# Keeping an order for PE and DVE in the first two attention blocks, products of ones in PE's first waits, and gathered blocks late in the banks of the scores

## The chip, the cores and the metric

The kernel runs on one core of one Trainium2 chip. The time is the device time of one execution in microseconds. Before the change the median of three runs is 336.43 us (335.42 to 338.63). A profile is one more execution, recorded by the hardware.

The engines are named as in the profile: PE multiplies matrices, PEld is its load of the stationary operand, DVE works on vectors and reduces, ACT evaluates functions and copies, POOL does element-wise work and issues indirect DMAs, SP issues most other DMAs. SPq, ACTq, POOLq and PEq are their queues of instructions.

## The reference

A tensor x of shape (2, 1024, 256) passes through four residual steps, in float32. The context has 77 rows of 192 numbers for each of the two batches.

```python
x = x + L0_xattn(layernorm(x), ctx)   # 16 heads of 16, softmax over 77 keys
x = x + L0_ffn(layernorm(x))          # 256 -> 1024 -> 256, relu; then a layernorm
x = x + L1_xattn(layernorm(x), ctx)   # one head of 256
x = x + L1_ffn(layernorm(x))          # one of 8 matrices 256x256 for each position
```

In the first ffn only expert 0 counts, since its router weights are set to one for expert 0 and to zero for the others. In the last step the matrix of a position is the argmax of a product of its position code with the signs of `tile_sigs`: it depends on the position and the inputs, not on x.

## The kernel before

The 2048 rows of x are cut into eight chunks of 256 rows (`c` = 0 to 7), and each chunk into two blocks of 128 rows for the first attention (`b` = 0 to 15). The first four chunks are batch 0, the others batch 1. A chunk goes through four generators:

- `attention0` takes moments of x (`st_a`, `mv_a`, the root on POOL as `rs_a`, `sh_a`), normalizes on ACT (`n_a`), transposes on PE (`ps_xT_a`, copied by ACT to `xT_a`), forms `qT` by `ps_q`, and begins two blocks. `attention0_block` forms scores of all 16 heads in `sc`, a tile of four PSUM banks from the pool `ps2`, which has one buffer. DVE takes the maximum (`mx`) and subtracts it (`pr`) for each half of the heads, ACT takes the exponential, DVE sums (`sm`), takes reciprocals, and ACT spreads them (`sme`). PE transposes `pr` and `sme` in three banks of four (`ps_pT`), ACT copies them (`pT`), PE multiplies by the values (`ps_o<-pT,vbd`), DVE scales (`oT`), PE projects (`ps_y<-wo,oT`), and DVE adds to x.
- `ffn0` normalizes again (`n_f`), transposes, forms four pairs of hidden tiles (`ps_h`, `hT`), and sums them for the two blocks (`ps_eo`), and does the layernorm (`st_g`, `tb`).
- `attention1` is the second attention (`n_b`, `xT_b`, `ps_s`, `ps_pT1`, `ps_y` by `vo`).
- `to_slots` normalizes (`mv_h`, `rs_h`) and scatters the rows to `slots`, a buffer in HBM for each batch that is sorted by matrix, so that a block of 128 slots needs one matrix. The last chunk doesn't go there: `by_every_tile` multiplies it by all eight matrices (`ps_z`) and keeps the right one.

`block(e, j, place)` handles block j of 128 slots of batch e; there are 15 for batch 0 and 13 for batch 1. SP loads its matrix (`wt`, four buffers; for batch 1 ahead of time into the places of `vbd`, `w1`, `w2`) and its rows (`blk`, six buffers). PE transposes the rows (`ps_yT`), ACT copies (`yT`), PE multiplies (`ps_t`), DVE adds the bias (`res`), and POOL scatters to the output (`out<-res,blk`). Both PSUM tiles come from the pool `ps1`, which has four banks and serves all other products.

The order is set in two layers. Each generator yields places, numbers on a common scale of chunks, and `run` takes the generators from a heap by place. Within `run`, the instructions of the engines that are named in `ordered` keep the order in which they are issued; those of other engines, and all of them in a later `run` without names, are placed by the planner of the programming layer. It also adds every semaphore, and gives each engine one fixed order of instructions. Before the change DVE alone keeps its order, for places below 0.

Other generators in the first stage are `first_context` (keys: `ps_cxT`, `ps_k`, `kbd`), `values` (`ps_v`, the masked values `vbd`), `row_of_biases` (`bvb`, `ps_bv`, into `rows`), and `choices` (the matrix of each position; it needs `sigT` and `peT`). DMAs in `loads` that are issued late wait for the first transposes of chunk 0, done["a0"].

## Time and profile before

| | |
|---|---|
| median of three runs | 336.43 us |
| the profiled execution, its own time | 340.51 us |
| its span, first to last instruction | 338.4 us |
| PE busy | 301.8 us, 89%, 2144 instructions |
| DVE busy | 211.0 us, 62% |
| ACT busy | 141.4 us, 42% |
| POOL busy | 130.6 us, 39% |
| mean granted clock of PE | 0.967 |
| chain that ended last: PE, DVE, issue, DMA | 63%, 18%, 7%, 4% |
| moved by DMA | 39.69 MB, mean 117 GB/s |

The page shows the span in 40 slices of 8.46 us; a digit is the busy share of an engine in tenths, and PEclk the granted clock in tenths of full speed. A line of the timeline reads: start, busy time, engine, line of the kernel, operation, what it writes and reads, shapes, how often, and in brackets the idle time of the engine before it with what released it. Each float32 matmul that is not a transpose appears as two instructions. Matmuls are pipelined and their ends are modelled.

### The profile page before, as it was taken

The numbers are of one execution on the slowest core, as the hardware profiler recorded it, in microseconds if no ns is written. First come the engines' busy times: TensorE is split into PE (matmuls) and PEld (weight loads), VectorE is DVE, ScalarE is ACT, GpSimd is POOL, SyncE is SP. The second block draws the span as 40 slices with busy tenths as digits, with TensorE's granted clock in tenths as the row PEclk, the third lists the DMA queues.
The fourth block names the chain that finished last, engine by engine and source line by source line (L and its number), as shares of the span: only waits on it lengthen the run. The fifth ranks groups of instructions, "written<-read, shape, count | busy, mean of one in ns | idle before, by whom it ended". The sixth has DMA issues, their size and how long they took to land.

```text
span 338.4 us, 6080 instructions
## 1 busy us (share of the span) xinstructions
PE 301.8 (89%) x2144; PEld 247.6 (73%) x2144; DVE 211.0 (62%) x624; ACT 141.4 (42%) x309; POOL 130.6 (39%) x183
## 2 busy tenths in 40 slices
PE   2979789999799899999999999999799996578995
PEld 2656568888488678877887888888688885455884
DVE  2278884695459657929757784894346659326343
ACT  2246566535234457365464744645324421212110
POOL 3104560424003458346435512432652716415422
PEclk9999999999899999999999999999999999559999
DMA  7597299999401302701000100250845687164510
GB/s 198 197 334 184 104 241 139 213 158 76 39 0 44 115 13 93 255 32 45 20 2 0 64 0 2 69 182 1 252 133 183 204 253 254 64 186 128 167 34 16
DMA packets 23209, 39.69 MB, mean 117 GB/s; under 512 B 2669, under 2 KB 9354, under 8 KB 23180
## 3 DMA queue, kind: packets, MB, share of 16 engines
q1 hardware_dynamic: 19788, 32.22, 38.3%
q0 software_dynamic: 2848, 6.57, 5.9%
q10 hardware_dynamic: 544, 0.52, 0.5%
q8 instruction: 17, 0.28, 0.4%
q14 instruction: 12, 0.10, 0.1%
HBM read 25.52 MB, written 15.62 MB: 122 GB/s over the span
## 4 chain that ended last, share of the span: by engine, by line
PE 63%; DVE 18%; issue 7%; DMA 4%; POOL 3%; ACT 2%; SPq 1%; POOLq 0%; ACTq 0%
PE ps_eo L688 15%; PE ps_h L676 11%; PE ps_t L809 5%; PE ps_pT L634 4%; PE ps_z L834 4%; PE ps_y L656 4%; DVE mx L608 3%; PE ps_q L580 3%; DVE pr L610 3%; PE ps_o L643 2%; PE ps_s L721 2%; PE sc L599 2%; PE ps_y L746 2%; DMA wt<-in_wrow 2%; DMA wk<-in_wk 2%
## 5 line engine op out<-in xcount | busy, mean ns | idle before, releaser
L676 PE MATMUL ps_h<-xT_f,w 128*128 128x256 f32 x256 | 63.3, 390 | 3.0 <-issue 2.1
L688 PE MATMUL ps_eo<-w,hT 128*128 128x256 f32 x256 | 58.4, 381 | 1.9 <-ACT hT L681 1.9
L676 PEld LDWEIGHTS ps_h<-xT_f,w 128*128 128x128 f32 x256 | 47.0, 192 | 11.6 <-issue 4.5
L688 PEld LDWEIGHTS ps_eo<-w,hT 128*128 128x128 f32 x256 | 47.5, 190 | 8.3 <-ACT hT L681 2.3
L173 POOL DMA_INDIRECT out<-res,blk x28 | 27.4, 980 | 38.1 <-DVE res L814 14.5
L681 ACT ACTIVATE hT<-ps_h,cols 128x256 f32<-128x256 f32 x64 | 27.1, 466 | 30.7 <-PE ps_h L676 30.6
L614 ACT ACTIVATE pr<-pr 128x616 f32<-128x616 f32 x32 | 22.9, 717 | 37.5 <-DVE pr L610 37.5
L608 DVE TENSOR_REDUCE mx<-sc 128x8 f32<-128x616 f32 x32 | 25.2, 788 | 5.3 <-PE sc L599 5.3
L635 ACT COPY pT<-ps_pT 128x512 f32<-128x512 f32 x48 | 25.4, 595 | 6.2 <-PE ps_pT L634 6.2
L750 DVE SCALAR_TENSOR_TENSOR x<-ps_y,sm,x 128x256 f32<-128x256 f32 x16 | 7.1, 479 | 29.7 <-PE ps_y L746 29.7
L617 DVE TENSOR_REDUCE sm<-pr 128x8 f32<-128x616 f32 x32 | 24.6, 781 | 1.4 <-ACT pr L614 1.0
L610 DVE TENSOR_TENSOR pr<-sc,mx 128x616 f32<-128x616 f32 x32 | 25.2, 787 | 0.2
L805 ACT COPY yT<-ps_yT 128x256 f32<-128x256 f32 x28 | 10.4, 371 | 35.2 <-PE ps_yT L803 35.2
L634 PE MATMUL ps_pT<-ident,pr 128*128 128x128 f32 x160 | 21.0, 274 | 3.7 <-ACT pr L614 2.0
L566 POOL TENSOR_TENSOR x<-x,rows 128x512 f32<-128x512 f32 x16 | 21.0, 1321 | 8.3 <-ACT n_a L227 5.4
L634 PEld LDWEIGHTS ps_pT<-ident,pr 128*128 128x128 f32 x160 | 18.1, 141 | 5.9 <-ACT pr L614 2.5
L656 PE MATMUL ps_y<-wo,oT 128*128 128x256 f32 x64 | 17.4, 394 | 4.5 <-DVE oT L650 4.5
L765 POOL TENSOR_TENSOR both<-x,bias 128x256 f32<-128x256 f32 x14 | 9.9, 725 | 24.6 <-DVE x L750 24.5
L643 PE MATMUL ps_o<-pT,vbd 128*32 128x128 f32 x512 | 19.0, 283 | 0.1
L643 PEld LDWEIGHTS ps_o<-pT,vbd 128*32 128x32 f32 x512 | 14.4, 112 | 5.7 <-issue 4.5
L809 PE MATMUL ps_t<-wt,yT 128*128 128x256 f32 x60 | 16.9, 403 | 1.8 <-ACT yT L805 1.3
L173 POOL DMA_INDIRECT slots<-both,to x14 | 14.3, 1019 | 9.2 <-DVE both L232 2.7
(196 smaller groups left out, 545.8 us busy)
## 6 DMA issues: line engine op xcount, KB each, us to landing
blk<-slots SPq DMA_DIRECT2D x28, 256.5 KB
slots<-zero SPq DMA_DIRECT2D x1, 3847.5 KB
wt<-in_wrow SPq DMA_DIRECT2D x15, 256.0 KB
slots<-zero SPq DMA_DIRECT2D x1, 3334.5 KB
w<-in_w SPq DMA_DIRECT2D x2, 1024.0 KB
every<-in_wrow SPq DMA_DIRECT2D x1, 2048.0 KB
wt_w<-in_wrow SPq DMA_DIRECT2D x8, 256.0 KB
x<-in_x SPq DMA_DIRECT2D x7, 256.0 KB
```

The lines of the kernel that those rows point to most:

```text
L173: i = nc.gpsimd.indirect_dma_start(out=to, out_offset=bass.IndirectOffsetOnAxis(ap=index, axis=0), in_=rows_in, in_offset=None, bounds_che ...
L608: nc.vector.tensor_reduce(mx, scv, AX.X, ALU.max)
L610: nc.vector.tensor_tensor(p8.rearrange("p (j h l) -> p j h l", j=4, l=L), scv, mx.unsqueeze(3).to_broadcast([P, 4, 2, L]), ALU.subtract,)
L617: nc.vector.tensor_reduce(sm[:, g * 8 : g * 8 + 8], pr[:, g, :G8].rearrange("p (h l) -> p h l", l=L), AX.X, ALU.add,)
L634: nc.tensor.transpose(ps[:, j * P : (j + 1) * P], srcs[4 * n + j], ident)
L635: nc.scalar.copy(pT[:, n].rearrange("p j t -> p (j t)"), ps)
L643: nc.tensor.matmul(ps[32 * m : 32 * m + 32, g * P : (g + 1) * P], vbd[:, e, n, g, 32 * m : 32 * m + 32], pTs[:, g * NK + n, :], start=n == ...
L656: nc.tensor.matmul(ps[:, :D], oT[:, g, :], wo[:, g, :], start=g == 0, stop=g == KC - 1)
L676: nc.tensor.matmul(ps[:, j, :], w1[:, k, (f + j) * P : (f + j + 1) * P], tT[:, k, :], start=k == 0, stop=k == KC - 1,)
L681: nc.scalar.activation(hT[-1][:, j, :], ps[:, j, :], AF.Relu, bias=col(C_B1 + f + j))
L688: nc.tensor.matmul(ps[:, :D], hT[f // 2][:, f % 2, i * P : (i + 1) * P], w2[:, f, :], start=f == 0, stop=f == F // P - 1,)
L809: nc.tensor.matmul(ps[:, :D], yT[:, k * P : (k + 1) * P], w[:, k * D : (k + 1) * D], start=k == 0, stop=k == KC - 1,)
```

## The change

It moves and adds work and removes none of the results.

- PE and DVE both keep the order of issue, for all places below 1 instead of DVE for places below 0. Places of the first two chunks' generators are set by hand: `attention0(1)`, blocks 0 and 1 (`FIRST`), `values`, `row_of_biases`; `ffn0(0)` is placed 1.2 earlier.
- `warm` multiplies `ones` by itself 7, 5 and 2 times at three early places.
- In each block of the first attention the transposes of `pr` (banks 0 and 1) are placed ahead of the sums, and bank 2, with `sme`, after them.
- The load of `sigT` goes from SP's queue to ACT's.
- A block of slots no longer takes two banks from `ps1`. All 28 blocks use one tile `spare`, the four banks of the scores after their last use: block after block takes the next bank, transposes into its first half and multiplies into its second. Blocks of batch 0 are placed from 19.9 on, in steps of 0.1, instead of 16.0 in steps of 0.32. For batch 1 the place of the transposes is unchanged.

```diff
+    sigT = load("sigT", [NP, NT], a["sigT"], nc.scalar)
...
-    sigT = load("sigT", [NP, NT], a["sigT"])
...
+    def warm(n):
+        ps = bank(f"warm_{next(number)}")
+        for _ in range(n):
+            nc.tensor.matmul(ps[:, :P], ones, ones, start=True, stop=True)
...
     def attention0(c, x):
-        yield 2 * c - 1.8
+        at = {1: (-0.65, 0.04, 0.13)}.get(c) or (2 * c - 1.8, 2 * c - 1.4, 2 * c - 0.7)
+        yield at[0]
...
-            begin(2 * c + i, attention0_block(c, i, e, x, qT))
-        yield 2 * c + 1.2
+            begin({1: 0.12}.get(2 * c + i, 2 * c + i), attention0_block(c, i, e, x, qT))
+        yield 2 * c + 1.2 if c else 0.26
...
+    FIRST = {0: (0.1, 0.14, 0.3, 0.32, 0.34, 0.44), 1: (0.36, 0.37, 0.4, 0.42, 0.46, 0.5)}
     def attention0_block(c, i, e, x, qT):
+        at = FIRST.get(b) or (b + 0.45, b + 0.45, b + 0.5, b + 0.7, b + 1.1, b + 1.5)
...
-        yield b + 0.5
+        yield at[0]
+        pT_bank(0)
+        yield at[1]
+        pT_bank(1)
+        yield at[2]
...
-        yield b + 0.7
...
+        yield at[3]
+        pT_bank(2)
...
     def ffn0(c, x):
-        b = 2 * c
+        b = 2 * c if c else -1.2
...
+    spare = []
-    def block(e, j, place):
+    def block(e, j, place, late):
...
-        yield place + 0.8
-        ps = bank(f"ps_yT_{n}")
+        yield late
+        if not spare:
+            spare.append(ps2.tile([P, 4, 512], F32, tag="sc", name="spare"))
+        ps = spare[0][:, (e * NJ[0] + j) % 4, :]
...
-        yield place + 1.1
-        ps = bank(f"ps_t_{n}")
+        yield late + 0.05
+        ps = ps[:, KC * P :]
...
-        begin(2 * c + 2.7, ffn0(c, xs[c]))
+        begin(2 * c + 2.7 if c else 1.5, ffn0(c, xs[c]))
...
-    begin(1.1, once(row_of_biases))
-    begin(-0.3, paced(-0.3, 0.2, values()))
+    for place, n in ((-1.96, 7), (-1.56, 5), (-1.39, 2)):
+        begin(place, once(warm, n))
+    begin(-0.7, row_of_biases())
+    begin(0.02, values())
...
-            begin(place, block(e, j, place))
+            begin(place, block(e, j, place, (19.9, 21.6)[e] + (0.1, 0.17)[e] * j))
...
-    run(0, {mybir.EngineType.DVE})
+    run(1, {mybir.EngineType.PE, mybir.EngineType.DVE})
```

`pT_bank(n)` holds the four transposes and the copy of one bank, which stood in a loop over `n` before.

More of the change, by code (lines that the diff above doesn't have):

```diff
@@ L337, in values @@
         for c in range(NK):
-            yield
+            yield 0.2
             ps = bank(f"ps_v_{c}")
@@ L344, in values @@
             masked(0, c, ps[:, :D], nc.vector)
-        yield
+        yield 0.9
         none = work.tile([NK * P - G8, D], F32, tag="yT", name="none", bufs=3)
@@ L362, in row_of_biases @@
     def row_of_biases():
+        yield -0.7
         bvb = work.tile([P, KC, P], F32, tag="oT", name="bvb")
@@ L365, in row_of_biases @@
             nc.vector.tensor_scalar(bvb[:, k, :], ones, col(C_BV + k), None, ALU.mult)
+        yield 0.25
         ps = bank("ps_bv")
@@ L570, in attention0 @@
         m = moments(x, NI, f"a{c}")
-        yield 2 * c - 1.8
+        at = {1: (-0.65, 0.04, 0.13)}.get(c) or (2 * c - 1.8, 2 * c - 1.4, 2 * c - 0.7)
+        yield at[0]
         n = normed(x, NI, D, f"a{c}", m, act=True)
-        yield 2 * c - 1.4
+        yield at[1]
         xT = transposed(n, f"a{c}")
-        yield 2 * c - 0.7
+        yield at[2]
         qT = work.tile([P, KC, CH], F32, tag="qT", name=f"qT_{c}")
@@ L614, in attention0_block, with pT_bank @@
             nc.scalar.activation(p8, p8, AF.Exp, scale=1.0 / math.sqrt(HD))
-        yield b + 0.5
+        pT = work.tile([P, 3, 4, P], F32, tag="pT", name=f"pT_{b}")
+        srcs = [pr[:, g, n * P : (n + 1) * P] for g in range(KC) for n in range(NK)]
+        def pT_bank(n):
+            ps = bank(f"ps_pT_{b}_{n}")
+            for j in range(4):
+                nc.tensor.transpose(ps[:, j * P : (j + 1) * P], srcs[4 * n + j], ident)
+            nc.scalar.copy(pT[:, n].rearrange("p j t -> p (j t)"), ps)
+        yield at[0]
+        pT_bank(0)
+        yield at[1]
+        pT_bank(1)
+        yield at[2]
         for g in range(KC):
@@ L625, in attention0_block @@
         )
-        yield b + 0.7
-        pT = work.tile([P, 3, 4, P], F32, tag="pT", name=f"pT_{b}")
-        srcs = [pr[:, g, n * P : (n + 1) * P] for g in range(KC) for n in range(NK)]
+        yield at[3]
         srcs += [sme[:, g].rearrange("p h d -> p (h d)") for g in range(KC)]
-        for n in range(3):
-            ps = bank(f"ps_pT_{b}_{n}")
-            for j in range(4):
-                nc.tensor.transpose(ps[:, j * P : (j + 1) * P], srcs[4 * n + j], ident)
-            nc.scalar.copy(pT[:, n].rearrange("p j t -> p (j t)"), ps)
+        pT_bank(2)
         pTs = pT.rearrange("p n j t -> p (n j) t")
-        yield b + 1.1
+        yield at[4]
         ps = bank(f"ps_o_{b}")
@@ L652, in attention0_block @@
         )
-        yield b + 1.5
+        yield at[5]
         ps = bank(f"ps_y_{b}")
```

## The prediction

> **What bounds the kernel now.** I read the slices first, then the windows of the last stage, then the timeline.

> ```profile
> PE   2979789999799899999999999999799996578995
> DVE  2278884695459657929757784894346659326343
> ...
> PEclk9999999999899999999999999999999999559999
> ```

> PE is full from slice 6 to slice 34; what can be won lies before and after. Slices 35 and 36 show a half clock. By windows, late (columns: stretch, length, busy us and instructions of PE, PEld, DVE, ACT, POOL, then clock, DMA share, GB/s):

> ```profile
> 285.00:290.00 5.00, 1.07 (x6) 0.68 (x5) 4.53 (x34) 0.71 (x2) 2.16 (x3) 0.91 0.19 66
> 290.00:295.00 5.00, 4.63 (x16) 3.60 (x16) 0.43 (x2) 1.34 (x3) 2.70 (x3) 0.50 0.31 108
> 295.00:300.00 5.00, 1.39 (x5) 0.67 (x5) 1.42 (x5) 1.06 (x3) 0.00 (x0) 0.50 0.56 151
> 300.00:305.00 5.00, 5.00 (x14) 4.04 (x15) 1.78 (x5) 0.76 (x3) 1.47 (x2) 0.50 0.47 164
> ```

> PE idles 3.9 us, then 3.6, and its 11.0 busy us from 290 to 305 are at half clock: 5.5 too many. In this hole the last chunk passes through DVE alone. The first stage, and the two places in the middle that wait:

> ```profile
> 10.79 3.78 PE L580 MATMUL ps_q<-xT_a,wq 128*128 128x256 f32 x8 [0.68 <-ACT xT_a L257]
> 19.25 0.80 DVE L608 TENSOR_REDUCE mx<-sc 128x8 f32<-128x616 f32 x1 [0.29 <-PE sc L599]
> 29.07 1.99 PE L580 MATMUL ps_q<-xT_a,wq 128*128 128x256 f32 x8
> 48.79 1.89 PE L676 MATMUL ps_h<-xT_f,w 128*128 128x256 f32 x8
> 118.43 0.44 PE L634 MATMUL ps_pT<-ident,pr 128*128 128x128 f32 x2 [1.41 <-DVE x L657]
> 242.83 3.72 PE L688 MATMUL ps_eo<-w,hT 128*128 128x256 f32 x16 [1.94 <-ACT hT L681]
> ```

> The same eight matmuls cost 3.78 us at 10.79 and 1.99 at 29.07: PE starts cold, though the clock row says full speed there. What decides my forecast is one block of slots, alone on PE:

> ```profile
> 281.75 0.36 PEld L803 LDWEIGHTS ps_yT<-ident,blk 128*128 128x128 f32 x2
> 282.44 0.37 ACT L805 COPY yT<-ps_yT 128x256 f32<-128x256 f32 x1 [1.49 <-PE ps_yT L803]
> 282.86 1.13 PE L809 MATMUL ps_t<-wt,yT 128*128 128x256 f32 x4 [0.52 <-ACT yT L805]
> 283.61 0.35 PEld L803 LDWEIGHTS ps_yT<-ident,blk 128*128 128x128 f32 x2
> ```

> The next transpose starts 1.86 us after the last one and before the product has ended: it waits for no one. Each block has its own bank.

> [...] 3.78 against 1.99, and half clock after the 4.2 idle us ahead of 290.3. [...] n_b waits until 241.46 for sh_b, hT behind it on ACT comes at 241.96, and ps_eo waits 1.94. [...]

> **The change part by part.** Times on the clock of the trace before. What stands where, and which semaphore each instruction waits for, I take from the two built programs; durations from the trace.

> *Warm products.* 14 of 128x128, two passes each. A pass of a 128x128 transpose takes about 0.11 us warm and 0.22 cold (x4 in 0.44 and 0.87), so 14 cost 3 to 6 us, in PE's idle stretches to 3.96 and from 4.7 to 6.9. Seven cold ones end near 4.3: the first transposes start 0.3 late. If PE is warm by 7, ps_k (2.39), ps_xT (0.87) and ps_q (3.78) shrink to 1.05, 0.44 and 1.73: 3.8 us.

> *Order of the first blocks.* The scores of block 0 now stand ahead of ps_v (2.69). With the 3.8 us, the first mx of DVE moves from 19.25 to about 13.2. DVE then works in a row up to the statistics that the first ps_h needs: mx and pr of blocks 0 to 3 (15 of 0.79, 11.9), six sums (4.7), five vbd (2.1), and oT, rows, x, statistics, reciprocals (6.2): 24.9, with some 2.4 of waits for exp, scores and POOL's root. Then n_f, its transposes and their copy (2.5): ps_h starts at 43 instead of 48.79. But ps_q of chunk 2 (1.73) and block 2's transposes, ps_o, ps_y and xT (1.31, 1.05, 0.86, 0.44), 5.4 us, stood ahead of it and now stand behind: the head start is spent. Next, after chunk 0's second ps_eo, block 4's first transposes wait for this chain: tb, st_g, aggregate, tb (1.5), POOL's root (0.2 + 0.7 and hops: 1.1), x twice (0.9), mx, n_cx, pr (1.9), exp (0.8): 6.2 us. sc and ps_o cover 1.8; PE waits 4.4, then another 2.4 for the second half and sums. Before, PE was full from 60 to 85. Against 5.8 - 5.4 + 6.8 stand the 3.4 us lost at 89 to 95 (an idle 2.13 and cold matmuls), which I leave in half: **front +2 us**, bounds -6 and +5. sigT moves from SP (0.34 to issue) to ACT, which waits for x anyway: nothing. DVE's neg and sign (0.6) now stand ahead of the cxT copy: in the 0.3 to 0.5 late ps_k.

> *pT split.* In chunks 2 to 6 the transposes of pr go ahead of ps_y, those of sme behind ps_h. The waits there are 1.7 us for pT, 0.9 for hT, 1.5 for oT. Pulled forward after an even block, the second transposes meet exp 0.6 us early. **Middle -2.5**, bounds -4 and +1.

> *Blocks late, in the scores' banks.* All blocks share one tile of four banks. In the built program **every transpose of a block (from the third) waits for DVE's add of the block before it**, whatever bank it uses. So the chain of a block is: transpose to product 1.11 (281.75 to 282.86), product 1.13, add and its hops 0.52, sum **2.76 us** instead of 1.86. The add is read here:

> ```profile
> 321.96 1.03 PE L809 MATMUL ps_t<-wt_w,yT 128*128 128x256 f32 x4
> 323.03 0.42 DVE L814 TENSOR_TENSOR res<-ps_t,blk 128x256 f32<-128x256 f32 x1
> ```

> Queued behind the waiting transpose on PE: its own product, then the last chunk's matmuls; behind the add on DVE: the last chunk's roots. Now step by step.
> - hT stands ahead of n_b on ACT, so ps_eo of chunk 6 starts at 239.4, 3.4 us sooner.
> - Up to the end of chunk 7's ps_eo (277.45), eight products (0.86) and transposes (0.22) go: 8.6. New waits, where blocks covered copies and n_b: 2.5. It ends at 277.4 - 3.4 - 8.6 + 2.5 = 267.9.
> - Blocks 2 to 5 run in the chunk's DVE chain, which took 12.2 us (277.45 to n_b at 289.66). n_b at 280.1, transposed by 281.
> - Scores, products 6 and 7 and two waits for adds, to ps_y's end: 287.9. From there to xT_h 7.9 us as before (302.35 to 310.26): 295.8. Copy: 296.3.
> - Eight ps_z, each with a transpose and a product, 2.82 each as at 313 to 330: 22.6, to 318.9. The adds fit under the ps_z.
> - **Nine blocks of batch 1 are left.** Product 1.0, then eight chains of 2.76: 22.1, to 342.0. Before, these products lay between the ps_z.
> - Add 0.5, scatter to landing 2.7 (POOL 0.97 within it; the chain of waits shows DMA out<-res,blk 2.15), closing 0.4: 345.6 against 338.4. **Tail +7.2**, bounds -5 and +16.

> The loads don't bind: SP issues all in order, a block's load waits for the scatter six blocks earlier; from a product's end to the next transpose in that buffer I find 7.1 us (306.2 to 313.28) plus the block's own 2.2, against 6 x 2.76 = 16.6. As many loads, scatters and POOL instructions as before.

> **Sum**: +2 - 2.5 + 7.2 = +6.7 on the profiled execution's 340.51 gives 347.2. That execution lies 4.1 above the median of 336.43. If its half clock late is its own, the changed kernel, which has no such hole, keeps 347; if all of it ran long, 343. I take **346 us**, 2.8% above the median.

> **Rivals.**
> 1. *The chain binds, at full clock* (my forecast): 341 to 350. Chance 0.64.
> 2. *The chain cools PE.* In it PE works 1.08 warm us of 2.76, less than anywhere it stayed warm (1.08 of 1.86 at 279 to 286). At half clock a product takes 1.91 and a transpose 0.3 more: 8 x 1.2, 355. For it: the half clock at 290. Against: no single gap is over 1.3 us. 0.14.
> 3. *The head start lives.* If block 4's wait is absorbed, front and middle give 8 (their better bounds are 6 and 4): 340.5 - 8 + 7.2, less the same 1.2, 338.5: no change. Against it: 25 us of DVE work in a row. 0.14.
> 4. *The chain is not paid: faster.* Place: the nine blocks after the last ps_z. If they ran at 1.1 us, as at 306 to 309, where the next transpose overtakes the product, the tail is 13.3 shorter: 333, about 1% faster. It decides from a step of 1.6 us down. For it: four banks suffice for overlap. Against: the semaphores. 0.06.
> 5. *The products don't warm PE*, or the clock turns late: up to 4 us more, 350. 0.02, else inside 1.

> **Numbers.** About 1% (3.4 us) is what a measurement of this kernel tells from no change: its three runs span 3.2. Forecast 346; from rival 3's upper part to rival 2's lower: 338.5 to 354. Faster 0.06, within 1% 0.14, slower 0.80.

> **What would show it.** Right: ps_h's first near 43; a PE gap of 4 us ahead of block 4's transposes; no half clock at 290; xT_h near 296; after the last ps_z eight transposes some 2.8 us apart, each released by DVE res. Wrong: steps under 2 us there, or the last ps_z later than 325.

## The result, and the profile after the change

The changed kernel takes 371.5 us (median of four runs, 371.2 to 372.9), the kernel before 335.9 us beside it (335.1 to 338.6). The ratio is 1.105, with a 95% interval of 1.098 to 1.112. The profiled execution took 371.49 us; its span is 369.6 us (before 338.4) and its mean granted clock 0.906 (before 0.967). The forecast of 346 us had the sign, and about a quarter of the size. Medians are of all runs of a kernel; the ratios, here and below, leave out runs over 1.5% above the fastest of the same kernel.

The slices after the change, one digit for 9.24 us:

```profile
PE   8888499689999999999999999998996897996772
...
DVE  2686721577479597496576667645759335552010
...
PEclk9996679989999999999999999999998559999555
```

PE is busier at the start, as meant. But the clock row has three holes where the row before has one: slices 4 to 6, 32 and 33, and the last three. Windows from the three holes (length, busy us and instructions of PE, PEld, DVE, ACT, POOL, then clock, DMA share, GB/s):

```profile
40.00:50.00 10.00, 6.08 (x18) 4.53 (x19) 5.95 (x14) 5.50 (x11) 6.66 (x10) 0.52 0.00 0
...
290.00:300.00 10.00, 8.83 (x28) 6.59 (x28) 2.60 (x9) 2.92 (x7) 3.26 (x4) 0.50 0.74 200
...
340.00:350.00 10.00, 6.89 (x17) 3.69 (x17) 1.28 (x3) 1.12 (x3) 2.91 (x3) 0.54 0.34 97
```

From 290 to 300 us PE looks nearly full (8.83 us busy), yet it runs at half clock (0.50); a busy PE is not a fast one. The timeline of the front, the places that answer to those shown of before:

```profile
10.12 1.99 PE L589 MATMUL ps_q<-xT_a,wq 128*128 128x256 f32 x8 [0.23 <-ACT xT_a L257]
...
13.66 0.80 DVE L621 TENSOR_REDUCE mx<-sc 128x8 f32<-128x616 f32 x1 [1.17 <-PE sc L612]
...
43.23 1.39 PE L254 MATMUL ps_xT_f<-ident,n_f 128*128 128x128 f32 x4 [3.98 <-ACT n_f L227]
45.30 3.78 PE L696 MATMUL ps_h<-xT_f,w 128*128 128x256 f32 x8 [0.68 <-ACT xT_f L257]
...
74.90 1.33 PE L635 MATMUL ps_pT<-ident,pr 128*128 128x128 f32 x5 [4.21 <-ACT pr L627]
...
247.07 3.62 PE L708 MATMUL ps_eo<-w,hT 128*128 128x256 f32 x16
```

The products of ones work: ps_q takes 1.99 us (before 3.78), and DVE's first mx comes at 13.66 (19.25). Then PE waits 4.0 us for n_f; from 40.44 to 50.68 it is cold (a granted clock of 0.50), and it does the first ps_h at 45.30 in 3.78 us (1.89 before). At 74.90 it waits 4.2 us for exp of block 4. And the end of the timeline, behind the last ps_z:

```profile
338.08 0.44 PE L829 MATMUL spare<-ident,blk 128*128 128x128 f32 x2 [0.57 <-DVE res L840]
338.98 1.13 PE L835 MATMUL spare<-wt_w,yT 128*128 128x256 f32 x4 [0.46 <-ACT yT L831]
...
344.41 0.69 PE L829 MATMUL spare<-ident,blk 128*128 128x128 f32 x2 [0.58 <-DVE res L840]
345.56 2.07 PE L835 MATMUL spare<-wt_w,yT 128*128 128x256 f32 x4 [0.46 <-ACT yT L831]
348.21 0.69 PE L829 MATMUL spare<-ident,blk 128*128 128x128 f32 x2 [0.58 <-DVE res L840]
...
363.63 0.97 POOL L173 DMA_INDIRECT out<-res,blk  x1 [1.95 <-DVE res L840]
365.82 0.34 SPq L870 DMA_DIRECT2D out<-y  x1
```

This is the chain that was forecast: each transpose is released by DVE's add of the block before. Its step is first 2.60 us (335.48, 338.08, 340.69) and from 344.41 on 3.80 us.

Where the time went, by the same events on PE:

| event | before | after | later by |
|---|---|---|---|
| start of chunk 1's first ps_eo | 99.10 | 107.96 | 8.9 |
| start of chunk 5's second ps_eo | 222.00 | 229.66 | 7.7 |
| end of chunk 7's ps_eo | 277.44 | 276.95 | -0.5 |
| start of ps_xT_h, the last chunk's transposes | 310.26 | 309.72 | -0.5 |
| end of the last ps_z | 334.66 | 333.75 | -0.9 |
| end of the span | 338.4 | 369.6 | 31.2 |

So 8.9 us are lost in the front and 1.2 won back in the middle. The 8.2 us seemingly won ahead of chunk 7 are blocks that were not done: at ps_xT_h 20 of the 28 products of blocks were done in the kernel before, 11 in the changed one. The nine more that are left make the end.

### The profile page after: what moved, and what is told of

Same layout as the page of the kernel before. It is cut to its first block, busy times and chain, and to the rows that moved or that the text cites. A ratio compares the mean times of both kernels' runs of the same rounds, so it can differ in the third digit from the quotient of the medians.

```text
span 369.6 us, 6139 instructions
## 1 busy us (share of the span) xinstructions
PE 326.9 (88%) x2172; PEld 259.4 (70%) x2172; DVE 212.6 (58%) x624; ACT 141.3 (38%) x309; POOL 130.5 (35%) x183
## 4 chain that ended last, share of the span: by engine, by line
PE 56%; DVE 16%; issue 11%; POOL 7%; ACT 4%; DMA 3%; POOLq 1%; ACTq 0%; DVEq 0%; SPq 0%
PE ps_eo L708 13%; PE ps_h L696 11%; PE ps_pT L635 5%; POOL out L173 4%; PE ps_q L589 4%; PE ps_y L676 4%; PE ps_o L663 3%; PE spare L835 3%; DVE pr L623 3%; DVE mx L621 2%; PE ps_s L741 2%; PE sc L612 2%; PE ps_y L766 1%; DVE x L770 1%; DMA sigT<-in_sigT 1%
## 5 line engine op out<-in xcount | busy, mean ns | idle before, releaser
L696 PEld LDWEIGHTS ps_h<-xT_f,w 128*128 128x128 f32 x256 | 48.2, 195 | 8.9 <-issue 1.6
L831 ACT COPY yT<-spare 128x256 f32<-128x256 f32 x28 | 10.4, 373 | 64.7 <-PE spare L829 59.2
L840 DVE TENSOR_TENSOR res<-spare,blk 128x256 f32<-128x256 f32 x28 | 11.9, 425 | 39.1 <-PE spare L835 37.9
L636 ACT COPY pT<-ps_pT 128x512 f32<-128x512 f32 x48 | 26.9, 589 | 12.2 <-PE ps_pT L635 12.2
L635 PE MATMUL ps_pT<-ident,pr 128*128 128x128 f32 x160 | 26.0, 292 | 5.6 <-ACT pr L627 5.6
L635 PEld LDWEIGHTS ps_pT<-ident,pr 128*128 128x128 f32 x160 | 20.2, 150 | 9.6 <-ACT pr L627 7.1
L623 DVE TENSOR_TENSOR pr<-sc,mx 128x616 f32<-128x616 f32 x32 | 25.2, 788 | 0.2
L835 PE MATMUL spare<-wt,yT 128*128 128x256 f32 x60 | 20.9, 481 | 3.2 <-ACT yT L831 3.2
L829 PE MATMUL spare<-ident,blk 128*128 128x128 f32 x56 | 14.3, 346 | 8.6 <-DVE res L840 7.2
L829 PEld LDWEIGHTS spare<-ident,blk 128*128 128x128 f32 x56 | 7.2, 163 | 18.1 <-DVE res L840 17.1
L196 POOL TENSOR_SCALAR rs_g<-mv_g 128x2 f32<-128x2 f32 x6 | 1.6, 267 | 50.4 <-DVE mv_g L189 50.4
```

The costliest lines, as they stand in the source:

```text
L623: nc.vector.tensor_tensor(p8.rearrange("p (j h l) -> p j h l", j=4, l=L), scv, mx.unsqueeze(3).to_broadcast([P, 4, 2, L]), ALU.subtract,)
L635: nc.tensor.transpose(ps[:, j * P : (j + 1) * P], srcs[4 * n + j], ident)
L636: nc.scalar.copy(pT[:, n].rearrange("p j t -> p (j t)"), ps)
L696: nc.tensor.matmul(ps[:, j, :], w1[:, k, (f + j) * P : (f + j + 1) * P], tT[:, k, :], start=k == 0, stop=k == KC - 1,)
L835: nc.tensor.matmul(ps[:, :D], yT[:, k * P : (k + 1) * P], w[:, k * D : (k + 1) * D], start=k == 0, stop=k == KC - 1,)
```

## Experiments

All are timed beside the kernel before on the same chip; us is the median, and the ratio is to the kernel before, with its 95% interval. For e7, where two runs are left, no interval was formed: they took 345.7 and 344.6 us, beside 337.1.

| run | what is in it | us | ratio |
|---|---|---|---|
| e1 | front and split | 348.7 | 1.035 [1.027, 1.043] |
| e2 | blocks: common tile, late places | 353.5 | 1.047 [1.036, 1.059] |
| e3 | late places alone | 358.0 | 1.058 [1.048, 1.068] |
| e4 | split alone | 343.2 | 1.014 [1.004, 1.024] |
| e5 | common tile, places of before | 346.8 | 1.026 [1.015, 1.036] |
| e6 | late places, four separate banks | 342.0 | 1.010 [0.998, 1.022] |
| e7 | front without the split | 348.2 | none |
| e8 | products of ones alone | 335.5 | 0.993 [0.990, 0.996] |
| e9 | e7, chunk 0's ffn in its old place | 342.8 | 1.014 [1.007, 1.021] |
| e10 | the change with four separate banks | 350.4 | 1.041 [1.035, 1.047] |
| e11 | products of ones, four separate banks | 332.9 | 0.990 [0.984, 0.996] |
| e12 | e11, batch 0 somewhat later | 334.1 | 0.989 [0.986, 0.992] |
| e13 | the change, end of PE's order fixed | 364.2 | 1.077 [1.068, 1.086] |
| e14 | e13, two products per gap at the end | 364.5 | 1.077 [1.069, 1.085] |
| e15 | e11, products in chunk 7's waits | 330.6 | 0.978 [0.969, 0.987] |
| e16 | e13, two products per gap from 278 us on | 373.5 | 1.111 [1.104, 1.119] |
| e17 | e15 with more of them | 333.5 | 0.986 [0.979, 0.992] |

### The change in parts: e1 to e4

The theory was that the common tile of the blocks costs most, by the chain and the clock; the rivals were the front and the late places.

e1 puts the blocks back, e2 makes only their change:

```diff
-        yield late
-        if not spare:
-            spare.append(ps2.tile([P, 4, 512], F32, tag="sc", name="spare"))
-        ps = spare[0][:, (e * NJ[0] + j) % 4, :]
+        yield place + 0.8
+        ps = bank(f"ps_yT_{n}")
```

> The changed kernel with the blocks of slots as before (two banks of the common pool each, batch 0 from 16.0 on in steps of 0.32): only the order of the first two attention blocks, the warm products and the split of the transposes are left of the change. Theory A (the common tile of the blocks costs most of the time, by a chain through DVE's add and by PE's cooled clock): the front keeps the loss that the trace of the changed kernel shows (eo_0 of chunk 1 about 8 us later than before), the middle gives 1 to 3 us back, the tail is that of the kernel before: 339 to 345 us. Theory B (the new order of the front costs most, because it keeps the clock at half from 26 to 50 us and everything later is pushed): 355 to 372 us. Theory C (the front's loss in the trace was only work moved forward): 331 to 337 us.

> The kernel before with the change of the blocks alone: one tile of four banks for all of them, and the late places. Theory A (common tile): the last nine blocks follow the last ps_z one by one, 2.6 to 3.8 us each, the transposes released by DVE res; 352 to 362 us. Theory B (the front costs most): 334 to 345 us. My prediction's tail of +7.2 us at full clock would give 341 to 346 us.

e3 changes only the places of before, e4 only the order of transposes and sums:

```diff
-            begin(place, block(e, j, place))
+            begin(place, block(e, j, place, (19.9, 21.6)[e] + (0.1, 0.17)[e] * j))
```

```diff
+        yield at[0]
+        pT_bank(0)
+        yield at[1]
+        pT_bank(1)
+        yield at[2]
```

> The kernel before with the late places of the blocks alone; each block still takes two banks of the common pool of four. Theory A (the common tile): with two banks of its own a block's transposes wait for no other block, so blocks run at 0.7 to 1.9 us each and none is left over for a chain at the end: 328 to 340 us. Rival D (the late place itself, with nine blocks left for the end whatever bank they use): a tail of nine blocks at 1.2 to 2 us each after the last ps_z, 345 to 360 us.

> The kernel before with the split alone: in each attention block the transposes of pr ahead of the sums, those of sme after them. As predicted for the middle (-2.5 us, bounds -4 and +1): 332 to 337 us. If the split is what made block 4 wait for exp in the changed kernel: 338 to 342 us, with a gap of 3 to 4 us ahead of a ps_pT on PE before 110 us.

e1 and e2 add 10.8 and 15.5 us to the 337.9 beside them; e1 lies above the 339 to 345 that the theory gave. Together they add 26.3, and the whole change 35.6: the other 8 to 9 (7.8 by the ratios) are interaction. e4 missed: from chunk 2's first ps_eo to chunk 5's second the split gives nothing (92.17 us in the profile before, 92.13 here), and it loses in the front, where chunk 0's first ps_eo comes at 66.23 instead of 60.68. What it gives lies earlier in the middle: from chunk 1's first ps_eo to chunk 5's second the profile before takes 122.90 us and e4's 122.17.

e3 missed by 18 us, and it seemed to overturn the theory: late places alone, with no common tile, cost 20 us. Rival D's range holds it, but no block is left behind the last ps_z, as D had it. In its timeline 16 products of blocks run between chunk 7's second ps_eo and its ps_y, and from 289.5 to 320.2 PE is cold, at a granted clock of 0.50 (start, busy time, and in brackets the idle time before):

```profile
288.51 1.13 PE L809 MATMUL ps_t<-wt,yT 128*128 128x256 f32 x4 [2.20 <-ACT yT L805]
...
290.59 2.08 PE L809 MATMUL ps_t<-wt,yT 128*128 128x256 f32 x4 [0.52 <-issue]
...
327.63 0.60 PE L254 MATMUL ps_xT_h<-ident,n_h 128*128 128x128 f32 x4
```

PE has one order, and the blocks stand ahead of the last chunk in it. Its ps_xT_h comes at 327.6 instead of 310.3. So places and banks had to be taken apart.

### Places against banks: e5, e6, e10

e5 keeps the common tile and takes the places of before. e6 and e10 give the scores' space back and take it again as four tiles; the semaphores then reach back to the add four blocks earlier.

```diff
-            spare.append(ps2.tile([P, 4, 512], F32, tag="sc", name="spare"))
-        ps = spare[0][:, (e * NJ[0] + j) % 4, :]
+            scores.close()
+            spare.append(ctx.enter_context(tc.tile_pool(name="ps3", bufs=4, space=PSUM)))
+        ps = spare[0].tile([P, 512], F32, tag="spare", name=f"spare_{n}")
```

> The kernel before with the common tile of four banks for all blocks, but with the places of before (16.0 on in steps of 0.32): the serial chain without the lateness. Theory A' (the chain through DVE's add of the common tile costs the time wherever it stands): with 28 blocks at 2.6 us or more one after the other, 345 to 358 us, as with late places. Theory L (the late places cost the time, since 26 blocks then stand behind the last ps_eo with little other work between them): the blocks of batch 0 are covered by ps_h and ps_eo, only those of batch 1 wait for each other, 336 to 344 us.

> The late places, with four separate tiles of one bank each in place of the common tile of four banks (the scores' space is given back and taken again as four tiles), so that a transpose waits only for the add four blocks before. Theory A': without the chain the tail falls back to that of before or less, 328 to 341 us; no row of spare transposes released by DVE res of the block before. Theory L: the time stays with the late places, 345 to 358 us, as the two kernels with late places so far (353.5 and 358.0).

> The changed kernel with four separate tiles of one bank each in place of the common tile; front, split and late places as in the change. If chain and clock of the common tile are worth in the whole change what they were alone (353.5 against 342.0) or more, since here the chain also ran cold: 350 to 360 us. If front and tail losses only add up and the cold chain is something else: 360 to 366 us. If the banks are not the matter: 369 to 373 us.

| us | pool of four banks, two per block | common tile | four separate banks |
|---|---|---|---|
| places of before | 337.9 | 346.8 | not alone; e11's ratio is 0.003 below e8's, within the intervals |
| late places | 358.0 | 353.5 | 342.0 |
| late, with front and split | not run | 371.5 | 350.4 |

The common tile costs 11.5 us at the late places and 21.1 in the whole change. Late places with banks of their own (e6) are within the interval of no change, 1 us above what was expected without the chain. With the pool they are bad for another reason: e3 differs from e6 in that each block takes two of the four banks that all other products use. The groups of transposes at the late places, e2 first and e6 below (busy us and mean ns, then idle time before them with its releasers):

```profile
L807 PE MATMUL spare<-ident,blk 128*128 128x128 f32 x56 | 12.4, 301 | 9.0 <-DVE res L818 8.8
```

```profile
L809 PE MATMUL spare<-ident,blk 128*128 128x128 f32 x56 | 10.3, 292 | 7.2 <-DMA blk<-slots 6.6 <-DVE t_h L211 0.6
```

With separate banks the waits for the add are gone. In their place stands the load of the rows, which I had said doesn't bind. At the steps of the chain it hardly does (1.1 us in all in the changed kernel); where e6 does blocks in bursts, one behind the other in about 1 us, it does. That new wait may be what the late places still cost; no run takes it away.

### The front: e7 to e9

e7 is the front without the split and with the blocks of before. e8 adds only the three groups of products of ones to the kernel before. e9 is e7 with one thing undone:

```diff
-        b = 2 * c if c else -1.2
+        b = 2 * c
...
-        begin(2 * c + 2.7 if c else 1.5, ffn0(c, xs[c]))
+        begin(2 * c + 2.7, ffn0(c, xs[c]))
```

> The order of the first two blocks and the products of ones alone: transposes of pr and sme together again behind the sums, blocks of slots as before. If losses add up (front and split together 348.7, split alone 343.2, before 337.9): 342 to 345 us. If the split is what makes block 4 wait (4.2 us ahead of its transposes in the front): 336 to 340 us. If the hand-set order alone carries the whole loss of the front: 347 to 350 us.

> The kernel before with the 14 products of ones alone, ahead of ps_cxT, ps_k and ps_xT. By the trace of the changed kernel ps_k, ps_xT and ps_q then take 3.8 us less and DVE's first mx starts 3 to 4 us sooner. If the front is a chain from there: 331 to 335 us. If the gain is lost again in PE's waits further on, or the clock falls again behind them: 336 to 340 us.

> The order of the first two blocks and the products of ones alone (as in the run before, 348.2 us), but the first feed-forward of chunk 0 keeps its old place, so ps_xT_f and ps_h of chunk 0 stand again behind block 2's transposes, ps_o, ps_q of chunk 2 and ps_y. Theory F (the head start is spent by pulling ps_h ahead of chunk 2's attention: the same work then waits later for DVE's chain, 4.2 to 4.5 us ahead of block 4): 334 to 339 us, and eo_0 of chunk 1 starts at 93 to 98 us instead of 105.6. Rival G (it is the order of PE and DVE itself, scores of chunk 1 ahead of block 0's own work): the loss stays, 344 to 350 us.

e7 keeps most of the loss of e1: by its two runs it is 8 us over the kernel before, e1 11, and chunk 1's first ps_eo comes at 105.62 in its profile and at 107.81 in e1's (99.10 before). The products of ones alone win 0.7%, less than the 3.8 us they take out of the start: the first mx is at 15.25 us in that profile, 4.0 sooner than before, but the first ps_eo, at 59.52, only 1.2 sooner; between them PE waits 2.4 us for pT (42.4), and the ps_q behind it takes 2.86 us (1.99 at 25.07). The loss of the front is the order set by hand. e7's timeline:

```profile
41.33 1.40 PE L254 MATMUL ps_xT_f<-ident,n_f 128*128 128x128 f32 x4 [5.43 <-ACT n_f L227]
43.40 5.64 PE L690 MATMUL ps_h<-xT_f,w 128*128 128x256 f32 x16 [0.68 <-ACT xT_f L257]
...
72.58 2.07 PE L670 MATMUL ps_y<-wo,oT 128*128 128x256 f32 x4 [4.50 <-DVE oT L664]
```

ps_h is 5.4 us sooner than before, after an idle 5.4 that block 2 used to fill; then DVE sits idle for 7.0 us until ps_o of block 2, which now stands behind ps_h (its oT starts at 55.44); and PE pays 4.5 us at 72.58. With the ffn back in its place (e9) some 3 us return, by e9's ratio against e7's two runs, and 5 us of loss are left: the time falls between the two theories. The profiles show less: chunk 1's first ps_eo comes at 103.86, 1.8 us sooner than in e7, but e9's profile is its longest execution, 345.2 us. What is left stays with the order of PE and DVE. No run takes it apart; in e9's profile PE waits 2.6 us at 25.2 for qT of chunk 1 and 4.3 at 54.1 for oT. In the second wait DVE has one short instruction ahead of oT that ran for as long as POOL's additions beside it:

```profile
48.44 1.27 POOL L574 TENSOR_TENSOR tb<-n_f,rows 128x512 f32<-128x512 f32 x1
48.51 3.76 DVE L232 TENSOR_SCALAR n_cx<-cx,mv_cx,rs_cx 77x192 f32<-77x192 f32 x1 [0.45 <-POOL rs_cx L197]
49.67 2.48 POOL L574 TENSOR_TENSOR x<-x,rows 128x512 f32<-128x512 f32 x2
```

The same instruction takes 0.37 us at 57.22. So some 3.4 of the 4.3 us come from this one instruction; why it was held is not shown.

### The clock: e13, e14, e16

e13 issues the last nine blocks behind the ps_z and keeps PE's order there, to have a base that does not shift; e14 adds two products of 128x128 behind each of those blocks' own, e16 behind those of blocks 1 to 8 of batch 0. Their results are not used.

```diff
+            late = 24.4 + 0.1 * j if e and j > 3 else (19.9, 21.6)[e] + (0.1, 0.17)[e] * j
...
+        if late > 24:
+            fill = bank(f"fill_{n}")
+            for _ in range(2):
+                nc.tensor.matmul(fill[:, :P], yT[:, :P], ident, start=True, stop=True)
...
+    run(24.35)
-    run(math.inf)
+    run(math.inf, {mybir.EngineType.PE})
```

> The changed kernel with PE's order fixed by hand for the last nine blocks behind the last ps_z, as it stood in the changed kernel anyway: the base of the next run. Both theories: 369 to 374 us, the last nine steps partly at 2.60 and partly at 3.80 us.

> As the run before it, with two more products of 128x128 behind each block's own in the last nine blocks (0.44 us at full clock, in the gap in which PE waits for DVE's add; what they give is not used). Theory K (PE's idle share in the chain takes the clock): all steps stay at 2.60 to 2.70 us, 5 to 7 us less than the run before it. Rival H (the clock falls for another reason): no less time, steps of 3.8 us or more.

> As the pinned base (364.2 us), with two more products of 128x128 behind the product of each of the blocks 1 to 8 of batch 0, where the base goes at half clock from 282 to 303 us (what they give is not used; the order of two blocks against the last chunk's ps_s shifts by it). Theory K (PE's idle share takes the clock): no half clock there, steps of 2.60 instead of 3.80 us for six or seven blocks, 5 to 9 us less: 355 to 360 us. Rival H (the clock falls for another reason): steps stay at 3.8 us or more, 364 to 368 us.

e13 missed to the good side: the steps between its last nine blocks all stayed at 2.60 us (the first at 2.55), and it is 7.3 us faster than the changed kernel with nearly the same order. So e14 had nothing to give back and tells nothing. But the pair of e13 and the changed kernel shows what the clock is worth: five steps of some 3.80 instead of 2.60 us are 6 of the 7.3 us. Windows of 3.41 us, laid on the boundaries at which the clock changes, first the changed kernel, then e13:

```profile
337.40:340.81 3.41, 1.80 (x8) 1.00 (x8) 0.85 (x2) 0.37 (x1) 0.97 (x1) 1.00 0.39 131
340.81:344.23 3.42, 2.56 (x6) 1.27 (x6) 0.30 (x1) 0.37 (x1) 0.97 (x1) 0.50 0.54 168
344.23:347.64 3.41, 2.76 (x6) 1.46 (x6) 0.12 (x1) 0.37 (x1) 0.97 (x1) 0.50 0.34 83
```

```profile
340.07:343.49 3.42, 2.00 (x8) 1.08 (x8) 0.62 (x2) 0.46 (x2) 2.37 (x4) 1.00 0.40 105
343.49:346.90 3.41, 2.04 (x8) 1.32 (x9) 0.42 (x1) 0.65 (x2) 1.59 (x2) 1.00 0.63 192
```

The same chain keeps PE busy for 1.80 us of one window (53%), and the next is cold; at 2.00 and 2.04 (59 and 60%) it stays warm. Once cold, 2.76 of 3.41 us (81%) do not bring the clock back here, and the chain stays cold to the end: the clock is 0.50 from 340.81 on.

e16 agrees with theory K here, though its time missed. The base goes at half clock from 282 to 303 us. From 270 to 282 us e16 does the same work on PE in the same order, with the products added. The window ahead of the fall in e13, and the one that answers to it in e16:

```profile
278.63:282.05 3.42, 1.66 (x7) 0.88 (x6) 3.42 (x19) 0.47 (x3) 2.53 (x4) 1.00 0.47 146
```

```profile
279.39:282.80 3.41, 2.13 (x12) 1.48 (x10) 3.41 (x18) 0.37 (x1) 2.53 (x4) 1.00 0.46 133
```

At 1.66 us (49%) the clock falls, at 2.13 (62%) it stays, and the steps of the filled blocks are then 2.60 us at full clock:

```profile
288.05 0.44 PE L829 MATMUL spare<-ident,blk 128*128 128x128 f32 x2
288.95 1.13 PE L835 MATMUL spare<-wt,yT 128*128 128x256 f32 x4 [0.46 <-ACT yT L831]
289.91 0.61 PE L842 MATMUL fill<-ident,yT 128*128 128x128 f32 x4
290.65 0.44 PE L829 MATMUL spare<-ident,blk 128*128 128x128 f32 x2
...
305.84 0.41 PE L829 MATMUL spare<-ident,blk 128*128 128x128 f32 x2 [2.10 <-DMA blk<-slots]
```

Yet it lost 8 to 9 us against e13. Two more blocks went ahead of chunk 7's scores, and behind its ps_y PE waited 2.1 us for rows, and there the next three products of blocks took 2.07 to 2.08 us instead of 1.13. ps_xT_h came at 313.8 instead of 308.9, and nine blocks were again left for the end. What was won in the chain was not won on the path of the last chunk.

### A version that is better than both: e11, e12, e15, e17

e11 is the kernel before with the products of ones and the four separate banks at the places of before. e12 sets batch 0 later (17.4 on, in steps of 0.26). e15 adds products of 128x128 to e11, behind block 13 of batch 0 and behind chunk 7's ps_s; e17 has 24 instead of the 16.

```diff
+        if (e, j) == (0, NJ[0] - 2):
+            fill(16, yT[:, :P])
...
+        if c == NC - 1:
+            fill(6, xT[:, 0, :P])
```

> A version meant to be better than both: before with the products of ones (alone: 335.5 us) and four separate banks for the blocks, at the places of before. If the pool of four banks made products wait in the tail: 328 to 333 us. If only the loads and chunk 7's chain on DVE bind there: 333 to 337 us.

> As the run before it, but the blocks of batch 0 from 17.4 on in steps of 0.26 (16.0 and 0.32 before), so that four to six more products lie in the 8 idle us of the hole that chunk 7's chain leaves on PE, and out of the full stretch ahead of it. If the hole is filled: 4 to 6 us less than with the early places, 325 to 331 us, without the half clock behind 285 us. If the six buffers of rows make the later blocks wait for their loads: 333 to 340 us, with waits for blk<-slots ahead of transposes in the hole.

> The products of ones, four separate banks and the places of before (332.9 us), with 16 products of 128x128 ahead of the last chunk's ps_xT_b and 6 behind its ps_s, in stretches of 3.9 and 1.5 us in which PE waits for n_b and for exp (their results are not used). Theory K: no half clock from 283 to 298, ps_xT_b, ps_s, ps_pT and ps_y in 2.4 us less, 329 to 332 us. If the chain there is set by DVE and by the load of the first block of batch 1: 332 to 334 us.

> As the best version (330.6 us), with 24 products instead of 16 ahead of the last chunk's ps_xT_b, since 2.0 us of idle and 6.8 us of half clock were left there. Theory K: no half clock before the end, ps_xT_b to ps_pT 1 to 2 us less, 328 to 331 us. If the products now delay n_b's transposes: 330 to 333 us.

e11 is 1.0% faster than before; 0.7 of that the products of ones give alone, and what the separate banks add is within the noise. e12 fills the hole with blocks and wins nothing more: its transposes there wait for their rows, 3.8 us at 287.2. e15 fills it with products that need no rows. Of the 17 us of half clock ahead of 300 in e11's profile 6.8 are left, and it is the fastest, 330.6 us, though its interval still overlaps e11's. e17, with more of them, is not better than e15, and outside what was expected; the row load of batch 1's first block sets ps_y there (3.6 us of wait at 294.5), and its profile is cold from 20 to 31 us besides (ps_q takes 2.88 us at 28.71), where e11's is from 21 to 27.

## Why the prediction was wrong

Right were the sign and most of the places: the chain through DVE's add, nine blocks left behind the last ps_z, ps_z with transpose and product at 2.82 us each (2.81 measured), the 4.4 us ahead of block 4 (4.21), the first ps_eo of chunk 6 3.4 us sooner (3.5, with 7.7 us of shift taken off), four banks under one tile that give no overlap. Three of its marks failed: there was half clock at 290, ps_xT_h came at 309.7 (302.0 with the shift taken off) instead of near 296, and the last ps_z at 333.15, behind the 325 that was named as a sign of being wrong. The sum failed in two of its three terms, and the third was near for a reason not forecast.

**Tail, +7.2 forecast, 23.5 measured** (31.2 less 7.7). The failing step is "the chain binds, at full clock", with rival 2 set aside because "no single gap is over 1.3 us". That the clock goes by single gaps was the author's estimate: in the changed kernel it fell at 340.81, behind a window in which PE was busy for 1.80 of 3.41 us with no gap over 0.6. By the profile's records the chain keeps PE busy for 1.57 us of a step of 2.60. With the front's 7.7 us taken off, the forecast's own marks are missed thus: end of chunk 7's ps_eo +1.4; from there to ps_xT_h +4.9, where blocks and last chunk ran at half clock from 282 to 303 (how much of it the clock made is open, since e16 kept the clock there and came later still); the ps_z +0.9; last nine blocks +6.0, five cold steps; closing +3.1. These add to 16.3. The warm step itself was right, 2.60 against 2.76: in e2 the nine blocks took 0.4 us less than forecast. The closing is a wait that I had not seen: the store of y's second half stands behind the landing of the last scatter; both write the same tensor, which would be why. The scatter goes out at 363.63, the store at 365.82; the trace has SP waiting 21.3 us for scatters at that line.

**Front, +2 forecast, 8.9 measured.** The step that failed is "the head start is spent", as an even exchange of 5.8 for 5.4 us. Pulling ps_h ahead of chunk 2's attention cost some 3 us by e9 (in e7's profile DVE then runs dry for 7 us); and with the wait for n_f came a clock of 0.50, from 40.44 to 50.68: ps_h came at 45.3 instead of 43 and its first eight matmuls took 3.78 us. The sum was short in itself, too: of the terms that it names, 6.8 of waits less 0.4 of head start less half of the 3.4 are 4.7, not 2. Rival 3 (the head start lives) fell with it; the warm start alone holds and is worth 0.7% (e8).

**Middle, -2.5 forecast, -1.2 measured.** It is the split's: from chunk 1's first ps_eo to chunk 5's second the profile takes 122.91 us in e7, without it, and 121.70 in e1, with it, as in the changed kernel. But in chunks 2 to 6, where the forecast put the gain, there is none (e4), and alone the split loses more in the front. That the size came near is luck.

Rival 4 said that four banks would overlap if the chain were not paid. The changed kernel pays it; with separate tiles it is not paid (e6, e10), but late places then wait for rows.

What stays open: the part of the front's loss that e9 left, and the 8 to 9 us by which the whole change is slower than e1 and e2 together. The cold end explains 6 of these, since e2's chain went in steps of 2.60 us; why the changed kernel had a low clock in all four runs, which agree within 1.7 us (mean clock 0.906 to 0.914), was not shown.

## What to carry to other kernels

The planner here waits by tile: parts of one large tile share its waits, whichever banks they lie in (8.8 us of waits for the add in e2, none in e6), so cut the tile where the wait shall end. Cost a serial chain at the clock that it leaves: take PE's busy time per step, as the profile's records give it, over the step. Here that is 60%, and the clock was kept in e2 and e13 and lost in the changed kernel; at such a share, reckon with both. And of work pulled forward ask which engine's chain was fed by what it overtakes; filling a wait wins only on the path that sets the end.

## What the runs showed of the hardware

| busy share | windows at full clock | then half | windows at half clock | then full |
|---|---|---|---|---|
| under 0.45 | 4 | 4 | 3 | 0 |
| 0.45 to 0.70 | 14 | 5 | 7 | 0 |
| 0.70 to 0.80 | 8 | 0 | 3 | 0 |
| over 0.80 | 148 | 0 | 13 | 7 |

In the mixed row the share alone does not part them. The five that were followed by half clock are all of the changed kernel, from 23.37, 30.20, 37.03, 279.37 and 337.40 us on, busy for 50, 53, 60, 50 and 53%; two of the kernel before, from 36.47 and 241.27 on, busy for 50 and 54%, were followed by full. Nor does the longest gap: it is 0.57 us in the window from 337.40 on, 1.72 and 1.56 us in those two. At half clock none of the 13 windows under 80% was followed by full, and of the 13 over 80% seven were.

The chain of the last nine blocks took 2.60 us a step in e2 and e13 and, from 344.41 on, 3.80 in the changed kernel. In e13 its windows of 3.41 us from 336.66 to 353.73 are busy for 57 to 65% and at full clock; in the changed kernel the window from 333.99 on is busy for 70%, the next for 53%, and the one after that is cold. That it goes by where the windows cut the steps is the author's estimate from these shares.
